# Where the constant rows of attention keys come from, and what stands behind a router on VectorE

## The chip, the core and the metric

One core of a Trainium2 chip runs the whole kernel: TensorE (PE: matmuls, with its weight loads), VectorE (DVE), ScalarE (ACT), GpSimd (POOL), and SyncE (SP), whose queue issues every DMA of this kernel. Inputs lie in DRAM, tiles in SBUF (128 partitions) or in PSUM, where matmuls write. The metric is device time in microseconds (us), the median of several runs; the profile is of one execution.

## The reference: what is computed

Two batches of 256 tokens of width 256 go through four blocks. Each block adds a cross-attention over a context of 4096 tokens, then a self-attention, then a feed-forward part (often experts with a router). The change concerns block 2's end and block 3's cross-attention:

```python
q = split_heads(hidden_states @ q_w.T + q_b)       # 16 heads of 16
k = split_heads(context @ k_w.T + k_b)
v = split_heads(context @ v_w.T + v_b)
scores = einsum('bhqd,bhkd->bhqk', q, k) / sqrt(16)
scores = where(mask, -inf, scores)
ctx = einsum('bhqk,bhkd->bhqd', softmax(scores), v)
```

Block 2's feed-forward part has eight routed experts and two shared ones: the two largest of eight logits per token get softmax gates, the other experts a gate of zero.

## The kernel before

**Two lanes and a planner.** The program is written by two helpers ("lanes"): a on the left of SBUF, x on the right; the trace puts the lane's letter before a tile's name (axn, xk). The order on each engine is not the order of the program: a planner simulates the program on a timeline and puts each instruction where it expects it to be ready; explicit dependencies bind it. `behind` (a method that was there before) adds such a dependency: on the same engine it only orders, across engines it waits. Once planned, each engine runs its queue strictly in order.

**Block 2, batch 1.** `l2_attn` (L1234 its output) stacks keys and queries of heads by small DMAs (L526, the last at 846.74 us), then `l2_ffn` normalizes its output (`layernorm`: statistics L426 and L427, abn_ve L432, a power on GpSimd L417, axn L441), transposes it on TensorE (L449), copies it (axf L468, axnT), multiplies by the router (L1073), and finds the two largest logits and the gates in 19 small VectorE operations (`first_max` L1089 to L1097, up to L1262). `along` turns the gates (L1111) and spreads them over all partitions by way of DRAM (L1115, L1119). Five pairs of experts follow (`glu`: L413, L1028 to L1032, L1132 to L1135), then the output (L1269) and, in `x3_queries`, a second layernorm and the queries of block 3, written to DRAM (q_d).

**Block 3's cross-attention** (`l3_xattn`) works in two passes over the same keys. Keys and values were made earlier and lie in DRAM (kh_d and kl_d, the high and low part of a number in two, and v_d). A group is 4 heads of one batch: 8 groups, each in 4 chunks of 1024 keys, so 32 chunks. A chunk's keys are a tile of 128 partitions by 4 heads by 512: each half of the partitions holds 512 keys of each head, and in each half the 16 dimensions take four rows each: high, high, low, and one more (MASK, row 3 of each four). Of the sixteen rows of this kind in a half, the first (row 3) holds the mask of the keys and the others ones; the query tile has a one against row 3, and, in rows 7 and 11, two parts of minus the row's maximum against ones, so that the matmul itself adds the mask and subtracts the maximum. All other rows of this kind meet a zero in the query tile.

First pass (`max_steps`): per chunk eight times two matmuls into a PSUM tile f of two banks (L1378; two such tiles in turn), and a maximum over each 512 keys on VectorE (L1380, xpm<-xf). After a group's four chunks the maxima are joined (nm), turned and written into the query tile by DMA (`shift_rows`). Second pass (`exponents`): scores again (L1407), exponentials on ScalarE (L1411), times the values (L581). The first pass runs five chunks ahead (`ahead`): 40 maxima stand before the second pass begins, the other 216 are spread over it, eight a chunk. The scores of the second pass use PSUM buffers of the x lane and, in turn, those of lane a, in which block 2's experts and the queries of batch 1 work; the trace's first L1407 comes behind them.

**Tiles.** Seven key tiles (RING) and three query tiles (Q_SETS) are used in turn. `x3_tiles` fills each once: a key tile with ones by a memset on GpSimd (L1300), so that a chunk's loads need to bring only its keys (three loads, L1370) and its mask rows (L1371, row 3 of each half); a query tile with a copy of the column unmask (one in row 3 of each half, else zero) on GpSimd (L1296). Query rows come by six DMAs of 64 KB (L526), three for each half. The first four key tiles and the first query tile lie in a pool on the left (early), where lane a worked on batch 0's experts and queries until then; the others in a pool on the right (late).

`masks` runs in block 1, at about 460 us: it turns the mask into 0 or −1e30 in DRAM (md), spreads it over four heads (mk_d), and writes a small tile of ones to DRAM (fill_d).

Of the kernel before, what the change touches and what calls it, by code (L numbers as in the profile page):

```python
# [28 lines left out]
P = 128  # L29
# [261 lines left out]
class Lane:  # L291
# [231 lines left out]
    def rows_from(self, x, at, n, src, step=1):  # L523

        to = x[at : at + step * (n - 1) + 1 : step].bitcast(F32)
        self.nc.sync.dma_start(to, src.bitcast(F32) if src.dtype == F32R else src)  # L526
# [117 lines left out]
class Perceiver:  # L644
# [528 lines left out]
    def l2_attn(self, k, b, x):  # L1173
# [3 lines left out]
        with k.pool("a2", bufs=1) as ap:  # L1177
# [37 lines left out]
            for g in range(4):  # L1215
# [5 lines left out]
                k.rows_from(k4, k.ADD + 2, 2, sqd[:, g4, :])  # L1221
# [15 lines left out]
    def l2_ffn(self, b, x):  # L1237
# [4 lines left out]
        with k.pool("f2", bufs=2) as fp:  # L1242
# [19 lines left out]
            nc.vector.tensor_add(g8, g8, h2)  # L1262
# [21 lines left out]
    def x3_tiles(self, at):  # L1284


        k, nc = self.x, self.nc
        i, c = divmod(at, self.N_C)

        def tile(tag, n):  # L1290
            return k.t(self.early if at < self.N_C else self.late, [P, GRP, n], tag, F32R, bufs=1)

        if c == 0 and i < self.Q_SETS:

            x = tile(f"q{i}", S)
            nc.gpsimd.tensor_copy(x, self.unmask.unsqueeze(1).to_broadcast([P, GRP, S]))  # L1296
            self.x3_q.append(x)
        if at < self.RING:
            x = tile(f"k{at}", 512)
            nc.gpsimd.memset(x.bitcast(F32), 1.0)  # L1300
            self.x3_k.append(x)
        return self.x3_q[i % self.Q_SETS], self.x3_k[at % self.RING]
# [10 lines left out]
    def masks(self):  # L1313

        k, nc = self.a, self.nc
        with k.pool("mask", bufs=1) as mp:
# [10 lines left out]
            nc.sync.dma_start(self.fill_d, fill)  # L1327

    def x3_queries(self, b, x):
# [3 lines left out]
        with k.pool("x3q", bufs=1) as ap:  # L1333
            xnT = k.transposed(k.layernorm(x, ap), ap, "xnT")
            k.to_dram(k.proj_t_split(wq, xnT, ap, "qT", bias="x3.bq"), self.q_d[b])

    def l3_xattn(self, xs):
# [13 lines left out]

        def max_steps(at):
# [3 lines left out]
            g4 = slice(GRP * g, GRP * g + GRP)  # L1356
            q4, k4 = self.x3_tiles(at)
            if c == 0:
                for h in range(2):
                    at = h * self.HALF  # L1360
                    for r, part in enumerate(k.QUERIES):
                        src = self.q_d[b, part].rearrange("m (h d) n -> d (m h) n", d=HD)
                        k.rows_from(q4, at + r, HD, src[:, g4, :], self.PARTS)
                    if i >= self.Q_SETS:
                        k.rows_from(q4, at + self.SHIFT, 2, self.zeros, self.PARTS)
                state[i] = q4, k.t(self.early, [P, 2, GRP, 2 * n_c], "pm", bufs=2), []
            q4, pm, ks = state[i]
            u2 = slice(2 * c, 2 * c + 2)
            for r, src in ((0, self.kh_d), (1, self.kh_d), (2, self.kl_d)):
                nc.sync.dma_start(k4[r :: self.PARTS].bitcast(F32), src[b, u2, :, g4, :].rearrange("u d j n -> (u d) j n"))  # L1370
            nc.sync.dma_start(k4[self.MASK :: self.HALF].bitcast(F32), self.mk_d[b, u2])  # L1371
            ks.append(k4)
            for j in range(GRP):
                for t in range(2):
# [5 lines left out]
                    nc.vector.tensor_reduce(at, both.rearrange("p (h n) -> p h n", h=2), axis=AX.X, op=ALU.max)  # L1380
# [82 lines left out]
        nc.gpsimd.memset(self.zeros.bitcast(F32), 0.0)  # L1463
        xp = self.late
# [7 lines left out]
        for at in range(ahead):  # L1472
            steps = max_steps(at)
# [6 lines left out]
        for at in range(n):  # L1480
            steps = max_steps(at + ahead) if at + ahead < n else iter(())
# [356 lines left out]
    def run(self):  # L1838
# [15 lines left out]
        self.q_d = a.dram([B, 2, 2, P, S], "q_d")  # L1854
# [6 lines left out]
        self.v_d = a.dram([B, 4, P, L // 512, 4 * GRP * (HD + 1)], "v_d")  # L1861
        self.md = a.dram([B, L], "md")
# [13 lines left out]
        with ExitStack() as wa:  # L1876
            a.wraw = wa.enter_context(a.pool("wraw", bufs=2))
            a.wp = wa.enter_context(a.pool("w", bufs=4))
            with ExitStack() as early:
# [3 lines left out]
                with self.psum(x, mm=2, s=2, pr=1), self.psum(a, mm=3), x.pool("wraw", bufs=1) as x.wraw, x.pool("w", bufs=2) as wp, x.pool("xq", bufs=1) as self.xq:  # L1883
# [37 lines left out]
                    xb[1] = self.l2_attn(x, 1, xb[1])  # L1921
                x.p_bufs = 3
# [51 lines left out]
```

## Time and profile before

| what | us |
|---|---|
| median of 3 runs (lowest, highest) | 1518.61 (1515.18, 1522.23) |
| the profiled execution's own time | 1513.83 |
| its span, first to last instruction | 1512.1 |
| busy in the span: PE, DVE, ACT, POOL | 1353.1, 1108.8, 891.4, 521.0 |
| L1380, 256 maxima: busy, mean of one | 310.2, 1.234 |
| output of block 2's attention, batch 1 (L1234 begins) | 863.10 |
| first and last L1380 begin | 870.4, 1230.2 |
| first L1407 begins | 951.7 |

The page gives, of one execution, each engine's busy time; then the chain of waits, followed back from the last instruction, whose shares say what the end hung on. The timeline lists instructions of an engine in order of time: start, duration (of several merged ones, their whole stretch), engine, line, operation, output and input, and in brackets how long the engine sat idle before and for whom. A table by stretches gives, for each, its length and each engine's busy time (PE, PEld, DVE, ACT, POOL) with the number of instructions, the granted TensorE clock (1.00 is full speed), the share of time in which the 16 DMA engines were busy, and GB/s. An instruction that straddles two stretches counts in both numbers, its time only where it falls.

### The profile page before, as it was taken

How to read it: one execution, taken by the hardware profiler on the slowest of the kernel's cores; microseconds unless marked ns; L12 is line 12 of the kernel's file. 1: busy time of each engine (PE TensorE's matmuls, PEld its weight loads, DVE VectorE, ACT ScalarE, POOL GpSimd, SP SyncE). 2: the span in 40 equal slices, each digit the busy share in tenths (PEclk: the TensorE clock that was granted, in tenths of full speed). 3: DMA queues.
4: the chain of work that ended last, by engine and by line, in shares of the span. 5: the costliest groups of instructions: out<-in, count | busy, mean ns of one | idle time of the engine just before them, and what ended most of it. 6: DMA issues, size and time to landing. Idle time of an engine off the chain costs nothing.

```text
span 1512.1 us, 29306 instructions
## 1 busy us (share of the span) xinstructions
PE 1353.1 (89%) x11278; PEld 1108.8 (73%) x11278; DVE 1108.8 (73%) x1863; ACT 891.4 (59%) x1644; POOL 521.0 (34%) x397
## 2 busy tenths in 40 slices
PE   7898788979998999998998767899999998987698
PEld 6898778969998998998898436455555544774588
DVE  6999855446467878885588599799999961566675
ACT  6676555637775655764664303688888897233243
POOL 6755344335445544664335413000000001531130
PEclk9999999979999999999999959899999999986799
DMA  8754164556455556445642542333333312300262
GB/s 288 250 152 131 33 190 161 184 172 217 149 177 169 176 177 214 146 155 179 164 128 89 172 165 95 121 119 109 126 122 107 113 53 61 136 1 30 84 218 75
DMA packets 125143, 212.00 MB, mean 140 GB/s; under 512 B 12840, under 2 KB 89240, under 8 KB 121480
## 3 DMA queue, kind: packets, MB, share of 16 engines
q1 hardware_dynamic: 125004, 210.13, 44.1%
q8 instruction: 89, 1.46, 0.4%
q14 instruction: 50, 0.41, 0.1%
HBM read 181.32 MB, written 28.61 MB: 139 GB/s over the span
## 4 chain that ended last, share of the span: by engine, by line
PE 48%; DVE 14%; ACT 5%; DMA 4%; POOL 4%; issue 3%; SPq 1%; POOLq 0%; DVEq 0%; ACTq 0%
PE amm L413 9%; PE xacc L581 7%; PE xmm L413 6%; PE xf L1378 5%; DVE xpm L1380 4%; PE xs L413 4%; PE xpr L413 4%; DMA awr<-in_w 2%; PE amm L1407 2%; POOL aw L406 2%; ACT xp L1409 1%; PE xmm L788 1%; PE amm L1796 1%; PE xs L1407 1%; PE amm L581 1%
## 5 line engine op out<-in xcount | busy, mean ns | idle before, releaser
L1380 DVE TENSOR_REDUCE xpm<-xf 128x2 f32<-128x1024 f32 x256 | 310.2, 1234 | 7.5 <-PE xf L1378 5.9
L1411 ACT ACTIVATE xp<-amm 128x512 f32<-128x512 f32 x284 | 162.0, 595 | 29.6 <-PE amm L1407 17.6
L406 POOL TENSOR_TENSOR aw<-awr,aw 128x1024 fp32r<-128x1024 f32 (+1 forms) x53 | 126.5, 2389 | 148.2 <-ACT aw L404 114.8
L404 ACT CAST aw<-awr 128x1024 fp32r<-128x1024 f32 (+1 forms) x112 | 114.0, 1021 | 99.8 <-DMA awr<-in_w 60.3
L413 PE MATMUL xmm<-xvx,xpT 128*128 128x256 f32 x1152 | 167.2, 291 | 2.8 <-DVE xo L801 1.3
L581 PE MATMUL xacc<-xp,xv 128*17 128x256 f32 x2048 | 161.0, 387 | 4.1 <-DVE xot L1430 1.1
L413 PE MATMUL xs<-xkx,xqkT 128*128 128x256 f32 x1152 | 162.1, 285 | 2.7 <-POOL xkx L738 1.9
L738 POOL TENSOR_TENSOR xvx<-xraw,xvx 128x512 fp32r<-128x512 f32 x96 | 131.9, 1389 | 89.6 <-ACT xvx L736 89.1
L1378 PE MATMUL xf<-xk,xq 64*128 64x512 f32 x512 | 135.8, 527 | 22.2 <-DVE xpm L1380 13.6
L413 PEld LDWEIGHTS xmm<-xvx,xpT 128*128 128x128 f32 x1152 | 147.9, 193 | 6.0 <-DVE xo L804 2.0
L413 PEld LDWEIGHTS xs<-xkx,xqkT 128*128 128x128 f32 x1152 | 147.6, 191 | 4.6 <-POOL xkx L738 2.1
L1378 PEld LDWEIGHTS xf<-xk,xq 64*128 64x128 f32 x512 | 51.1, 196 | 124.1 <-issue 83.2
L407 DVE TENSOR_TENSOR aw<-awr,aw 128x1024 fp32r<-128x1024 f32 (+1 forms) x59 | 86.6, 1473 | 60.9 <-ACT aw L404 60.8
L1445 POOL TENSOR_TENSOR ax<-xou,xmh_ri 128x128 f32<-128x128 f32 x8 | 3.2, 402 | 315.9 <-DVE xmh_ri L1441 315.9
L413 PE MATMUL amm<-axnT,aw 128*128 128x256 f32 x636 | 98.9, 313 | 10.2 <-ACT axnT L404 5.5
L413 PE MATMUL amm<-ah,aw 128*128 128x256 f32 x768 | 99.6, 286 | 6.0 <-ACT au L1013 2.9
L413 PEld LDWEIGHTS amm<-axnT,aw 128*128 128x128 f32 x636 | 91.3, 217 | 17.8 <-ACT axnT L404 7.2
L413 PEld LDWEIGHTS amm<-ah,aw 128*128 128x128 f32 x768 | 94.7, 191 | 8.7 <-POOL aw L406 3.7
L738 POOL TENSOR_TENSOR xkx<-xraw,xkx 128x512 fp32r<-128x512 f32 x48 | 72.1, 1503 | 82.9 <-ACT xkx L736 82.3
L1411 ACT ACTIVATE xp<-xs 128x512 f32<-128x512 f32 x148 | 88.0, 595 | 11.3 <-PE amm L1407 7.8
L1407 PE MATMUL amm<-xq,xk 64*128 64x256 f32 x568 | 89.3, 283 | 3.0 <-DVE aqT L402 2.7
L777 ACT ACTIVATE xp<-xs,xnm 128x512 f32<-128x512 f32 x96 | 66.2, 690 | 34.8 <-DVE xnm L771 32.6
(603 smaller groups left out, 2920.6 us busy)
## 6 DMA issues: line engine op xcount, KB each, us to landing
awr<-in_w SPq DMA_DIRECT2D x105, 512.0 KB
xraw<-in_ctxT SPq DMA_DIRECT2D x108, 256.0 KB
xraw<-in_ctx SPq DMA_DIRECT2D x96, 256.0 KB
xk<-akh_d SPq DMA_DIRECT2D x64, 256.0 KB
av_d<-xkvv SPq DMA_DIRECT2D x16, 544.0 KB
xv<-av_d SPq DMA_DIRECT2D x32, 272.0 KB
akh_d<-xkvk SPq DMA_DIRECT2D x32, 256.0 KB
akl_d<-xkvk SPq DMA_DIRECT2D x32, 256.0 KB
```

Source lines behind the costliest of these rows:

```text
L404: nc.scalar.copy(dst.h, src)
L406: return lo.tensor_tensor(dst.l, src, dst.h.bitcast(F32), ALU.subtract)
L407: return nc.vector.tensor_sub(dst.l, src, dst.h)
L413: tie(self.nc.tensor.matmul(out, lhsT=x, rhs=y, start=start and i == 0, stop=stop and i == 2))
L581: inst = self.nc.tensor.matmul(acc[STRIP * j : STRIP * j + v(j).shape[1], :S], lhsT=v(j), rhs=p[:, j, :], start=start, stop=stop)
L738: nc.gpsimd.tensor_tensor(x.l, r, x.h.bitcast(F32), ALU.subtract)
L777: tie(nc.scalar.activation(p, score.pop(i), AF.Exp, bias=least[q], accum_out=su))
L788: tie(nc.tensor.transpose(pst[:, t * P : (t + 1) * P], p[:, t * P : (t + 1) * P], self.eye))
L1378: tie(nc.tensor.matmul(both[:, h * 512 : (h + 1) * 512], lhsT=q4[rows, j, t * P : (t + 1) * P], rhs=k4[rows, j, :], start=True, stop=True))
L1380: nc.vector.tensor_reduce(at, both.rearrange("p (h n) -> p h n", h=2), axis=AX.X, op=ALU.max)
L1407: tie(nc.tensor.matmul(ps[h][:, j, :], lhsT=ks[c][rows, a + j, s * P : (s + 1) * P], rhs=q4[rows, a + j, :], start=True, stop=True))
L1411: exps = [nc.scalar.activation(p[:, h, a : a + 2, :], ps[h], AF.Exp, scale=0.25) for h in range(2)]
```

## The change

Key tiles are no longer filled on GpSimd. A DRAM array mo_d holds, for the 4 chunks of batch 0, all 16 rows of the fourth kind: mask in the first, ones in the other 15; `masks` writes it by two more DMAs. Chunks that use a key tile for the first time (the first seven) load these 32 rows of 8 KB instead of the two mask rows. The copy into the query tiles goes from GpSimd to ScalarE.

The loads of keys get a function of their own, `load_keys`; for the first four chunks it is called before the first pass is set up (a first `yield None`, which `run` takes with `next(l3)` right after batch 1's attention of block 2), with an order: behind the last stacking DMA of that attention (`self.stacked`). The maxima of chunk 0 get an order behind the last addition of the gates (`self.gated`, of the latest `l2_ffn`, batch 1's), on the same engine.

The queries' array in DRAM is laid out by dimension, head and token, so that `x3_queries` writes it by four DMAs instead of one, and each part of a query tile is read by one DMA for both halves (three instead of six).

```diff
 l2_attn:
-                k.rows_from(k4, k.ADD + 2, 2, sqd[:, g4, :])
+                self.stacked = k.rows_from(k4, k.ADD + 2, 2, sqd[:, g4, :])
 l2_ffn:
-            nc.vector.tensor_add(g8, g8, h2)
+            self.gated = nc.vector.tensor_add(g8, g8, h2)
 x3_tiles:
-            nc.gpsimd.tensor_copy(x, self.unmask.unsqueeze(1).to_broadcast([P, GRP, S]))
+            nc.scalar.copy(x, self.unmask.unsqueeze(1).to_broadcast([P, GRP, S]))
...
-            x = tile(f"k{at}", 512)
-            nc.gpsimd.memset(x.bitcast(F32), 1.0)
-            self.x3_k.append(x)
+            self.x3_k.append(tile(f"k{at}", 512))
 masks:
+            n_u = 2 * self.N_C
+            nc.sync.dma_start(self.mo_d[:, 0], self.md[:1, : n_u * 512].rearrange("a (u n) -> (a u) n", n=512).unsqueeze(1).to_broadcast([n_u, GRP, 512]))
+            ones = self.fill_d[:1, :].unsqueeze(1).to_broadcast([n_u, HD - 1, GRP * 512])
+            nc.sync.dma_start(self.mo_d[:, 1:].rearrange("u d j n -> u d (j n)"), ones)
 x3_queries:
-            k.to_dram(k.proj_t_split(wq, xnT, ap, "qT", bias="x3.bq"), self.q_d[b])
+            qT = k.proj_t_split(wq, xnT, ap, "qT", bias="x3.bq")
+            for m in range(2):
+                for r in range(2):
+                    dst = self.q_d[b, r, :, HEADS // 2 * m : HEADS // 2 * (m + 1), :].rearrange("d h n -> h d n")
+                    self.nc.sync.dma_start(dst, qT.both[:, r, m, :].bitcast(F32))
 l3_xattn:
-        def max_steps(at):
+        def load_keys(at):
             b, g, c, i = place(at)
             q4, k4 = self.x3_tiles(at)
             if c == 0:
                 state[i] = q4, k.t(self.early, [P, 2, GRP, 2 * n_c], "pm", bufs=2), []
+            g4, u2 = slice(GRP * g, GRP * g + GRP), slice(2 * c, 2 * c + 2)
+            loads = []
+            for r, src in ((0, self.kh_d), (1, self.kh_d), (2, self.kl_d)):
+                loads.append(nc.sync.dma_start(k4[r :: self.PARTS].bitcast(F32), src[b, u2, :, g4, :].rearrange("u d j n -> (u d) j n")))
+            if at < self.RING:
+                loads.append(nc.sync.dma_start(k4[self.MASK :: self.PARTS].bitcast(F32), self.mo_d[u2].rearrange("u d j n -> (u d) (j n)")))
+            else:
+                nc.sync.dma_start(k4[self.MASK :: self.HALF].bitcast(F32), self.mk_d[b, u2])
+            if at < n_c:
+                for x in loads:
+                    k.behind(x, self.stacked)
+            state[i][2].append(k4)
+        def max_steps(at):
...
+                for r, part in enumerate(k.QUERIES):
+                    src = self.q_d[b, part, :, g4, :].unsqueeze(0).to_broadcast([2, HD, GRP, S])
+                    nc.sync.dma_start(q4[r :: self.PARTS].bitcast(F32), src)
...
-                    nc.vector.tensor_reduce(at, both.rearrange("p (h n) -> p h n", h=2), axis=AX.X, op=ALU.max)
+                    found = nc.vector.tensor_reduce(at, both.rearrange("p (h n) -> p h n", h=2), axis=AX.X, op=ALU.max)
+                    if b == g == c == 0:
+                        k.behind(found, self.gated)
...
+        for at in range(n_c):
+            load_keys(at)
+        yield None
```

## The prediction

> **What bounds the kernel now.** I read the page first (busy shares, chain), then the chain in order of time, then the stretch between block 2's attention on batch 1 and the steady loop of block 3, engine by engine.
>
> ```profile
> PE 1353.1 (89%) x11278; PEld 1108.8 (73%) x11278; DVE 1108.8 (73%) x1863; ACT 891.4 (59%) x1644; POOL 521.0 (34%) x397
> ...
> PE 48%; DVE 14%; ACT 5%; DMA 4%; POOL 4%; issue 3%; SPq 1%; POOLq 0%; DVEq 0%; ACTq 0%
> ```
>
> TensorE carries the chain over the whole, but POOL holds 4% of it. In order of time, its POOL pieces between 845 and 882 us are L1300 and L1296, from 859.0 to 873.7, but for 0.5 us: the fillings that the change removes. The same stretches by engine (busy us and instructions, then granted clock, DMA share, GB/s):
>
> ```profile
> 863.80:873.80 10.00, 1.32 (x4) 0.63 (x4) 9.88 (x7) 0.00 (x0) 9.91 (x9) 0.64 0.85 281
> 873.80:884.40 10.60, 7.33 (x20) 2.83 (x20) 9.75 (x11) 0.00 (x0) 0.70 (x1) 0.50 0.75 250
> 884.40:902.00 17.60, 12.39 (x40) 6.14 (x38) 17.37 (x35) 1.28 (x3) 0.00 (x0) 0.50 0.31 109
> 902.00:920.00 18.00, 16.35 (x96) 12.57 (x96) 16.02 (x18) 5.48 (x8) 3.68 (x2) 0.84 0.27 89
> 920.00:938.80 18.80, 16.68 (x109) 13.78 (x110) 18.03 (x23) 5.14 (x9) 6.59 (x4) 0.91 0.24 74
> 938.80:955.80 17.00, 7.75 (x40) 5.89 (x39) 7.49 (x14) 5.96 (x8) 5.40 (x3) 0.79 0.41 125
> ```
>
> The third busy column is VectorE. It is full from 863.8 to 938.8 us, but its first 10 us do nearly nothing (7 instructions), and from 938.8 to 955.8 every engine is below half. Its lines:
>
> ```profile
> 864.83 8.91 DVE L432 TENSOR_SCALAR abn_ve<-abn_mv 128x2 f32<-128x2 f32 x1
> 870.44 3.31 DVE L1380 TENSOR_REDUCE xpm<-xf 128x2 f32<-128x1024 f32 x2
> ...
> 883.71 0.73 DVE L441 TENSOR_SCALAR axn<-ax,abn_mv,abn_rs 128x256 f32<-128x256 f32 x2
> ...
> 901.68 0.17 DVE L1262 TENSOR_TENSOR ag<-ag,agh 128x16 f32<-128x16 f32 x1
> ```
>
> And GpSimd's:
>
> ```profile
> 858.98 7.03 POOL L1300 MEMSET xk<- 128x2048 f32 x4
> 865.96 0.56 POOL L627 MEMSET xot<- 128x256 f32 x2
> 866.47 1.03 POOL L1296 CAST xq<-ac_unmask 128x1024 fp32r<-128x1024 f32 x1
> 867.45 5.28 POOL L1300 MEMSET xk<- 128x2048 f32 x3
> 872.69 1.03 POOL L1296 CAST xq<-ac_unmask 128x1024 fp32r<-128x1024 f32 x1
> 873.82 0.70 POOL L417 TENSOR_TENSOR abn_rs<-abn_ve,amhalf 128x2 f32<-128x2 f32 x1
> ```
>
> Batch 1's layernorm for block 2's experts needs abn_ve (VectorE, two numbers a row), then a power on GpSimd (L417), then axn. abn_ve takes 8.91 us; the same instruction took 0.17 at 944.98. It ends with GpSimd's last filling (873.7). The power stands behind the fillings in GpSimd's queue anyway. By 873.8 the plan of the program has ten first maxima (L1380) ahead of axn, so axn is done at 884.4 instead of about 866.6; then each of the routing's small operations alternates with a maximum of 1.2 us, and the gates (L1262) are ready at 901.85. The experts follow (output at 940.84), then batch 1's queries, and the steady loop:
>
> ```profile
> 946.48 1.18 PE L449 MATMUL amm<-ac_eye,axn 128*128 128x128 f32 x4 [5.67 <-issue]
> 948.33 3.44 PE L413 MATMUL amm<-axnT,aw 128*128 128x256 f32 x12 [0.67 <-ACT axnT L404]
> 951.70 0.51 PE L1407 MATMUL amm<-xq,xk 64*128 64x256 f32 x1
> 954.92 0.50 PE L1407 MATMUL amm<-xq,xk 64*128 64x256 f32 x3 [2.71 <-DVE aqT L402]
> ```
>
> So two things must be finished before the loop can run (exponents, L1407): batch 1's experts and queries (whose PSUM buffers the scores reuse), and 32 of the 40 first maxima with their row shift. The maxima were finished by 938.8 and the experts were late: that is what the change can win, VectorE's idle time from 938.8 to 955.8.
>
> **Part by part.**
>
> *Fillings gone from GpSimd.* 7 memsets of 1.794 and 3 copies of 1.026: 15.6 us of GpSimd, and with them the wait of abn_ve and of the power. The Trainium skill, "SBUF — State Buffer", section "Who interferes with whom", names the cause: a tensor_scalar can take both ports, which GpSimd shares, and the second to come blocks for one whole instruction of the other. Here it blocked through the rest of one GpSimd instruction and seven more, 8.91 us, where by that rule it would be at most one, 1.79, and abn_ve alone would lose 7 us less. The sum needs no rule for it: the power's place in GpSimd's queue alone sets 873.8.
>
> *Routing runs alone.* By rows of this stretch: output of the attention 863.8; statistics to 864.8; abn_ve 0.17; power 0.70; axn 0.73, so 866.6; four transposes 1.1; copy on ACT 0.58; logits 1.88 (L1073); sum of these with gaps 870.2. Then 19 small VectorE operations that follow each other at 0.20 us (888.57 to 889.2), 3.8, and one exponential on ACT (0.20) with two handovers, about 0.7; with the gaps, gates at **874.9** instead of 901.85.
>
> *Maxima behind the gates.* The wait is on the eight maxima of chunk 0, but all others use the same two PSUM buffers (f), so all 40 stand behind 874.9. Behind the waiting maximum on VectorE stand the later maxima; on TensorE the third pair of their matmuls. Nothing else that could run is lost if the planned order puts the routing in front, which the dependency enforces on VectorE. What is lost are the 23 maxima that before ran up to 901.8. Their price: eight in a row take 9.14 us (874.65 to 883.79), 1.14 each; beside others 1.22. I take 1.18: 27.1 us.
>
> *The sum.* After the gates, VectorE before had 16.02 + 18.03 + 7.49 = 41.5 us of work up to the loop. After the change: 41.5 + 27.1 = 68.6 from 874.9, so 943.5 with no idle time. From 902 to 938.8 it idled 36.8 − 34.05 = 2.8; with as much, 946.3. I round to **946** for the state that before was reached at 955.8: 10 us won. Check on the other need: gates to output took 39.0 before, output to last query 14.1; from 874.9 that is 928. The 32nd maximum comes eight (9.1 us) before the end, 937; its shift (nm, split, transposes, ACT copy, DMA: 0.22 + 0.5 + 0.4 + 0.4 + two issues of 0.65 and about 2 to land) gives 942, so exponents begin while the last four maxima run. VectorE sets the end, not the chain.
>
> *Rows of ones by DMA.* A chunk's keys are three loads of 256 KB and 16 KB of mask (L1371); now the fourth load is 32 rows of 8 KB, 256 KB: 1.68 MB more for seven chunks, at the 322 to 341 GB/s of 865.9 to 873.8 some 5 us of a queue that is already 0.95 busy there. But keys no longer wait for fillings: the tiles' space comes free when batch 0's queries are in DRAM (855.4, where GpSimd's zeros waited for that write), against first loads at 864.0 before. Four chunks, 4.2 MB, take 12.6 us at 332 GB/s: 868 to 870. Maxima need them from 874.9: nothing, as long as TensorE's queue does not hold the routing behind them (first rival).
>
> *Moves with one answer, nothing:* q fillings on ACT (three of about 1.03, as L404's 128x1024 copies; ACT idles from 860 to 885.7); q_d written by four DMAs instead of one (three more issues of 0.38 on SP, which idles from 849.8 to 854.4); queries read by three DMAs instead of six (SP saves about 1.8 us a group; no wait for SP stands in the loop's chain).
>
> *mo_d is written at about 467 us*: two issues (0.70 each, as mk_d's) and 1 MB, between 0 (TensorE 9.45 of 10 busy, loads ahead) and 4.5 us (1.4 of issue and 3.1 of DMA, since one raw load was waited for 5.3 us there). I take **1**.
>
> *Clock.* TensorE idles from 863.1 to 869.5 before and was granted 0.61, then 0.50 up to 902; after, it again has little to do up to 874.9, then the experts' dense matmuls sooner. A pair of maxima's matmuls took 0.80 at 0.50, less than a maximum. Nothing. The Trainium skill, "TensorE: Matmul & The Clock Gate", section "What's actually happening", says a few us of idleness halve the clock and as much sustained work restores it; by it the expert matmuls of the first 3.4 us would take double, an estimate of 1.7 us against the change.
>
> Net 9: 1513.83 − 9 = 1504.8 on the profiled execution's scale (span 1512.1 and 1.7 around it). That execution lies 4.8 below the median 1518.61; I predict on the median's scale: **1509.6**.
>
> **Rivals.**
>
> *Late queries.* If q's loads are issued behind the four chunks' keys, they land at about 870.5 (868.0, 1.2 for 0.39 MB, and the landing); if TensorE's planned order has the first two pairs of maxima's matmuls (1.3) ahead of the routing's transposes, these start at 871.8 instead of 866.5 and the gates come at 880: 5 of the 9 lost, 1515. For it: the 25.9 us that axf's wait is put down to xk's load show that the routing stood behind the maxima before. Against: the planner now knows that they wait.
>
> *Given back.* VectorE's idle time only moves, or the loop waits for chunks 5 and 6, whose keys are 30% larger, or mo_d costs its 4.5: 1518. Against: seven chunks were in by 890 before; loop loads come a chunk ahead.
>
> *Slower: experts without maxima between.* Expert and query work comes first in the program, and if the plan lets it run alone, 40 maxima start late. Batch 0's experts and queries took 47 us from gates (802.4) to the write at 849.4: from 874.9 that is 922, then 32 maxima at 1.14 and 5 of shift: 963.5 against 954.9, with mo_d's 1: 9.6 slower, 1528. It decides when VectorE idles over 12.4 us (943.5 to 955.8) between the gates and the loop. Against: before, maxima alternate with every expert operation.
>
> **Numbers.** Forecast 0.58, late queries 0.18, given back 0.10, slower 0.14. Half a per cent (7.6 us) is about what a measurement of this kernel can tell from no change. Of the forecast 0.46 lies beyond it and 0.12 within; late queries and given back lie within; of the slower 0.12 beyond. Faster 0.46, same 0.42, slower 0.12. The range runs from all idle time used and none lost, 1513.8 − 12.4 = 1501, to 1521, which takes in "given back" and leaves out most of the slower case.
>
> **What would show it.** abn_ve at 0.2 us; no POOL work from 857 to 865 but a weight split; gates near 875 with no L1380 before them; L1380 without gaps from there; L1407 begins near 942; the last L1380 9 to 10 us earlier than 1231.4. Wrong if gates come after 885, if VectorE shows idle gaps over 12 us before the loop, or if the loop's maxima take longer each than now (275.2 us for 216).

## The result, and the profile after

The changed kernel is slower. Its median is 1542.07 us (1539.89 to 1545.36, four runs) against 1520.42 for the kernel before on the same chip: a ratio of **1.015**, 95% interval 1.0114 to 1.0185. A second measurement (e16) gave 1.0155, 1.0132 to 1.0178. The forecast was 1509.6 with a range up to 1521.

The profiled execution took 1543.79 us (span 1542.0). First the page after, its busy times and its chain:

```profile
PE 1364.2 (88%) x11278; PEld 1114.7 (72%) x11278; DVE 1103.6 (72%) x1863; ACT 896.0 (58%) x1647; POOL 506.6 (33%) x387
...
PE 43%; DVE 16%; DMA 9%; ACT 5%; issue 3%; POOL 3%; SPq 1%; POOLq 0%; DVEq 0%; ACTq 0%
```

GpSimd has 14.4 us less to do and VectorE 5.2 less, as the fillings' removal should give; TensorE has 11 more for the same 11278 matmuls (its granted clock is 0.93 over the whole, before 0.94). DMA has gone from 4% of the chain (6% in a second profile of before, e15) to 9% (9% in e16 too): more of the end hangs on transfers. The other shares say little, since two profiles of one kernel differ as much (PE 48% and 60% in the two of before).

The stretches that answer to those shown of before, in the same columns (the attention's tail in two rows, the routing, the experts' start, a hole, the experts, and the last of the forty first maxima):

```profile
846.00:864.00 18.00, 15.73 (x111) 9.15 (x110) 8.46 (x22) 9.30 (x17) 2.02 (x2) 1.00 0.49 138
864.00:878.50 14.50, 10.65 (x46) 6.46 (x46) 3.53 (x6) 5.33 (x8) 0.30 (x1) 0.69 0.93 334
878.50:895.20 16.70, 4.39 (x17) 2.99 (x16) 8.12 (x29) 4.21 (x6) 3.61 (x4) 0.50 0.68 225
895.20:908.50 13.30, 12.43 (x74) 10.11 (x74) 12.00 (x13) 3.88 (x6) 0.00 (x0) 0.81 0.59 192
908.50:922.20 13.70, 0.50 (x2) 0.19 (x2) 0.00 (x0) 0.41 (x1) 1.28 (x2) 0.57 0.39 136
922.20:953.20 31.00, 26.75 (x148) 21.49 (x148) 26.72 (x28) 8.37 (x11) 10.90 (x6) 0.80 0.24 65
953.20:980.60 27.40, 16.91 (x56) 8.32 (x56) 26.06 (x35) 3.78 (x6) 3.04 (x2) 0.66 0.31 95
```

The fifth row is the new thing: for 13.7 us hardly any engine computes (GpSimd 1.28 us, at the end), and DMA is busy only 0.39 of the time. VectorE's rows in the timeline say what stands around it:

```profile
880.29 0.17 DVE L432 TENSOR_SCALAR abn_ve<-abn_mv 128x2 f32<-128x2 f32 x1
881.27 2.78 DVE L441 TENSOR_SCALAR axn<-ax,abn_mv,abn_rs 128x256 f32<-128x256 f32 x2 [0.82 <-DMA arow_f2.br<-in_rows]
...
894.98 0.17 DVE L1262 TENSOR_TENSOR ag<-ag,agh 128x16 f32<-128x16 f32 x1
895.15 2.36 DVE L1399 TENSOR_REDUCE xpm<-xf 128x2 f32<-128x1024 f32 x2
...
907.26 1.21 DVE L1399 TENSOR_REDUCE xpm<-xf 128x2 f32<-128x1024 f32 x1
922.22 0.69 DVE L1135 TENSOR_TENSOR au<-amm,ag 128x512 f32<-128x512 f32 x1 [13.74 <-POOL ag L1134]
```

The routing did what was forecast: abn_ve takes 0.17 instead of 8.91, the gates (L1262) come 15.9 us after the attention's output (879.2) instead of 38.1, with no maximum (L1399 now) ahead of them. Then VectorE waits 13.74 us for GpSimd's L1134, the multiplication of an expert's output by its gates. The gates go to all partitions by way of DRAM: SP's write L1115 and, once it has landed, its reads L1119. Of the kernel before, and then of the kernel after with the GpSimd and TensorE instructions that wait (two timelines):

```profile
904.46 0.30 SPq L1115 DMA_DIRECT2D agates<-agrow  x1
905.78 0.81 SPq L1119 DMA_DIRECT2D agates<-agates  x2
```

```profile
906.51 0.39 SPq L1115 DMA_DIRECT2D agates<-agrow  x1
916.46 0.81 SPq L1119 DMA_DIRECT2D agates<-agates  x2
920.92 1.26 POOL L1134 TENSOR_TENSOR ag<-ag,agates 128x512 f32<-128x512 f32 x1 [37.01 <-DMA agates<-agates]
922.96 2.29 PE L413 MATMUL amm<-axnT,aw 128*128 128x256 f32 x9 [13.92 <-DVE au L1135]
```

Before, 1.3 us lie between issuing the 8 KB write and issuing the reads that need it; after, 10.0. The write is also issued 11.4 us after L1262 (before 2.6): SP's queue still had loads of keys, values and queries ahead of it.

**Where the time went.** Both kernels were profiled twice (e15 and e16 are unchanged copies). Means of two profiles, us, by the same landmarks:

| stretch | before | after | difference |
|---|---|---|---|
| start to masks (L1324, L1322) | 468.8 | 473.1 | +4.3, the same work in both |
| masks to the end of block 2's attention on batch 0 (L1234) | 318.6 | 323.3 | +4.7 |
| to the end of the same on batch 1 | 77.8 | 83.0 | +5.2 |
| to the steady loop of block 3 (first L1407, now L1429, that writes lane x's score buffers, xs) | 91.7 | 102.4 | +10.7 |
| to the last maximum | 275.7 | 275.3 | −0.4 |
| to the end | 279.4 | 281.4 | +2.0 |

The first row is not put down to the change: up to there every engine runs the same instructions in the same order in both kernels, and over all eighteen profiles this point lies anywhere from 465.7 to 475.1, with no clear relation to the edits. The three rows in the middle are the question. (The very first L1407 writes a buffer of lane a, a little earlier; the table of before gives that one, 951.7. Counted to it, the way from the attention takes 87.9 before and 101.3 after.)

### The profile page after: what moved, and what is told of

Same layout as the page of the kernel before. It is cut to its first block, busy times and chain, and to the rows that moved or that the text cites. A ratio compares the mean times of both kernels' runs of the same rounds, so it can differ in the third digit from the quotient of the medians.

```text
span 1542.0 us, 29272 instructions
## 1 busy us (share of the span) xinstructions
PE 1364.2 (88%) x11278; PEld 1114.7 (72%) x11278; DVE 1103.6 (72%) x1863; ACT 896.0 (58%) x1647; POOL 506.6 (33%) x387
## 4 chain that ended last, share of the span: by engine, by line
PE 43%; DVE 16%; DMA 9%; ACT 5%; issue 3%; POOL 3%; SPq 1%; POOLq 0%; DVEq 0%; ACTq 0%
PE xacc L581 7%; PE amm L413 7%; PE xf L1397 5%; PE xmm L413 5%; DVE xpm L1399 5%; PE xs L413 3%; PE xpr L413 3%; DMA awr<-in_w 3%; PE amm L1429 2%; POOL aw L406 1%; ACT xp L1431 1%; PE xmm L788 1%; PE xs L1429 1%; DVE aw L407 1%; ACT aw L404 1%
## 5 line engine op out<-in xcount | busy, mean ns | idle before, releaser
L1399 DVE TENSOR_REDUCE xpm<-xf 128x2 f32<-128x1024 f32 x256 | 309.1, 1220 | 5.7 <-PE xf L1397 3.9
L1433 ACT ACTIVATE xp<-xs 128x512 f32<-128x512 f32 x148 | 88.0, 595 | 11.4 <-PE amm L1429 8.3
L1429 PE MATMUL amm<-xq,xk 64*128 64x256 f32 x568 | 88.8, 284 | 0.0
```

The costliest lines, as they stand in the source:

```text
L1399: found = nc.vector.tensor_reduce(at, both.rearrange("p (h n) -> p h n", h=2), axis=AX.X, op=ALU.max)
L1429: tie(nc.tensor.matmul(ps[h][:, j, :], lhsT=ks[c][rows, a + j, s * P : (s + 1) * P], rhs=q4[rows, a + j, :], start=True, stop=True))
L1433: exps = [nc.scalar.activation(p[:, h, a : a + 2, :], ps[h], AF.Exp, scale=0.25) for h in range(2)]
```

## The experiments

Ratios are against the kernel before on the same chip, with 95% intervals. The table holds stretches of each profile in us: A from masks to attention 0's end, B from there to attention 1's end, then abn_ve, the gates after attention 1's end with the maxima ahead of them, the write-to-read time of the gates (L1115 to L1119), and the loop after attention 1's end. A maximum counts as ahead when it begins before the record of the gates' last addition ends; the single one of e3, e8 and e11, where the order holds, begins within that record's last 0.1 us. Each profile is of one execution, which can lie several us off its run's median (e5's 7.3 and e7's 9.9 under it).

| run | ratio | A | B | abn_ve | gates (maxima ahead) | L1115 to L1119 | loop |
|---|---|---|---|---|---|---|---|
| before | 1 | 319.0 | 78.2 | 8.91 | 38.1 (24) | 1.3 | 91.6 |
| e15 before, again | 0.9993 [0.9978, 1.0009] | 318.2 | 77.4 | 8.83 | 38.0 (24) | 1.3 | 91.8 |
| after | 1.015 [1.0114, 1.0185] | 323.2 | 83.5 | 0.17 | 15.9 (0) | 10.0 | 102.5 |
| e16 after, again | 1.0155 [1.0132, 1.0178] | 323.4 | 82.5 | 0.17 | 16.2 (0) | 10.3 | 102.3 |
| e1 before, mo_d written | 1.0033 [1.0016, 1.005] | 322.1 | 79.2 | 8.22 | 37.4 (24) | 1.3 | 91.3 |
| e2 after, chunks 4 to 6 later | 1.0093 [1.0063, 1.0123] | 324.2 | 80.9 | 0.17 | 16.2 (0) | 10.1 | 94.7 |
| e3 before, order | 1.0039 [1.0021, 1.0058] | 321.0 | 77.3 | 7.89 | 17.2 (1) | 1.7 | 92.6 |
| e4 after, no order | 1.0062 [1.0038, 1.0086] | 323.3 | 81.8 | 0.17 | 28.6 (14) | 7.0 | 89.4 |
| e5 before, fillings behind gates | 1.0027 [1.0004, 1.0051] | 317.6 | 78.9 | 0.17 | 18.4 (8) | 1.3 | 88.5 |
| e6 before, fillings behind axn | **0.9962** [0.9941, 0.9983] | 317.3 | 77.3 | 0.17 | 22.7 (13) | 1.6 | 83.9 |
| e7 after, no order, no mo_d, old query path | 1.0013 [0.9988, 1.0039] | 318.1 | 78.1 | 0.85 | 23.4 (7) | 2.6 | 89.5 |
| e8 after, old query path | 1.0051 [1.0032, 1.007] | 323.7 | 77.3 | 0.85 | 17.7 (1) | 5.1 | 88.8 |
| e9 after, query reads by halves | 1.0035 [1.0018, 1.0052] | 321.9 | 83.3 | 0.17 | 11.9 (0) | 4.0 | 84.9 |
| e10 before, new query path | 1.0033 [1.0018, 1.0049] | 320.3 | 81.0 | 3.35 | 32.3 (24) | 1.3 | 86.9 |
| e11 = e6 and the order | 1.002 [1.0003, 1.0038] | 319.9 | 77.2 | 0.17 | 13.4 (1) | 1.6 | 86.4 |
| e12 before, ScalarE fills | 1.0037 [1.0016, 1.0059] | 315.6 | 85.7 | 0.17 | 23.0 (17) | 1.3 | 83.3 |
| e13 = e9 without mo_d | 1.0022 [1.0004, 1.0039] | 319.6 | 82.4 | 0.17 | 15.8 (0) | 1.6 | 88.1 |
| e14 = e9 without the order | 1.0 [0.9983, 1.0018] | 321.1 | 83.7 | 0.17 | 24.1 (14) | 1.3 | 83.5 |

**e1_written: mo_d's price.** Before, and `masks` also writes mo_d, which nobody reads.

```diff
 masks:
+            nc.sync.dma_start(self.mo_d[:, 0], self.md[:1, : n_u * 512].rearrange("a (u n) -> (a u) n", n=512).unsqueeze(1).to_broadcast([n_u, GRP, 512]))
+            ones = self.fill_d[:1, :].unsqueeze(1).to_broadcast([n_u, HD - 1, GRP * 512])
+            nc.sync.dma_start(self.mo_d[:, 1:].rearrange("u d j n -> u d (j n)"), ones)
```

> The kernel before, with the array mo_d allocated and written in block 1 as in the change, and read by nobody. Four-places theory (the change loses some 10 us by 490 us, 5 us at the end of block 2's attention and 19 us at the gates' spreading, and wins 22 at the routing): writing mo_d costs 3 to 4 us at about 480 us, and if the array's place in DRAM is what slows the weight loads from 250 us on, 7 more: 1520.4 + 3 to 10, so 1523 to 1531. Order theory (the loss is VectorE held idle, since first maxima may not run ahead of the gates): nothing here, 1520.

It cost 0.33%, 5.0 us (2.4 to 7.6). Most of it can be seen at one place. ScalarE and TensorE of before, and then of e1:

```profile
480.81 0.62 ACT L736 CAST xkx<-xraw 128x512 fp32r<-128x512 f32 x1 [5.25 <-DMA xraw<-in_ctxT]
482.27 1.69 PE L413 MATMUL xpr<-xw,xkx 128*128 128x256 f32 x12 [2.67 <-ACT xkvv L386]
```

```profile
485.94 0.62 ACT L736 CAST xkx<-xraw 128x512 fp32r<-128x512 f32 x1 [8.42 <-DMA xraw<-in_ctxT]
487.41 2.93 PE L413 MATMUL xpr<-xw,xkx 128*128 128x256 f32 x12 [5.84 <-ACT xkvv L386]
```

The load of context that before came 5.25 us late comes 8.42 late; TensorE idles 3.2 longer, and its next twelve matmuls take 1.2 longer (granted clock 0.65 from 484 to 490 us, before 1.00 there and from 479 to 485). Stretch A averages 322.9 in the eight profiles with mo_d (321.1 to 324.2) and 318.7 in the ten without (315.6 to 321.0): 4.2 us.

**e2_gates_first: are the later key loads in the gates' way?** After, and the key loads of chunks 4 to 6 stand behind the gates' reads.

```diff
+            elif at < self.RING:
+                for x in loads:
+                    k.behind(x, self.spread)
```

> The changed kernel, with the loads of chunks 4, 5 and 6 ordered on SP behind the DMA that spreads batch 1's gates. Four-places theory: the gates' way through DRAM falls from 23 us (897.8 to 920.9) to about 8, TensorE's gap of 13.9 us at 909 goes, 14 us won: 1528. Order theory: VectorE is as idle before the gates as in the change, and the maxima are as late: 1540 to 1542.

The write is issued sooner (2.7 us after the gates instead of 11.4), and 0.57% comes back. But its readers still follow 10.1 us later, with no key load around it: the packets in flight in that time are the queries', two at a time (e9 shows how to tell them). So the key loads explain when the write is issued, not how long it takes.

**e3_order_only and e4_no_order: the order.** Before with the order of the first maxima added, and after with it taken out.

```diff
-            nc.vector.tensor_add(g8, g8, h2)
+            self.gated = nc.vector.tensor_add(g8, g8, h2)
...
-                    nc.vector.tensor_reduce(at, ...)
+                    found = nc.vector.tensor_reduce(at, ...)
+                    if b == g == c == 0:
+                        k.behind(found, self.gated)
```

> The kernel before, with only the order of chunk 0's maxima behind the gates; GpSimd's fillings stay, keys and queries come as before. Four-places theory: abn_ve still ends with the fillings (873.7), then the routing runs alone, gates at about 884 instead of 901.9; 68.6 us of VectorE's work and 3 idle end at 955, where the loop began before: 1517 to 1523. Order theory: VectorE loses some 10 us before the gates and gives them to nobody: 1530 or more.

> The changed kernel without the order of the maxima behind the gates. Four-places theory: maxima may run between the routing's operations again, but keys and queries are still loaded ahead of the gates' spreading, so the 10, 5 and 19 us stay: 1536 to 1546. Order theory: the loss goes, 1520 to 1525.

By itself the order brings the gates 21 us forward (17.2 us after the attention instead of 38.1, though abn_ve still takes 7.89), and all of it is given back: the loop comes 92.6 us after the attention, before 91.7; the time is 0.39% longer. Without it, the changed kernel wins 0.9%. So neither of the two theories stated with e1 holds alone: the order has a price, and with it gone 0.62% of loss is left.

**e5_fill_later and e6_fill_behind_axn: keep the fillings, but out of the way.** Before, and GpSimd's fillings of all tiles but the first of each kind stand behind the gates (e5), or behind axn (e6, whose diff for the keys is shown; e5 has self.gated for self.normed, and the copies into the query tiles are treated alike); nothing else of the change.

```diff
-            nc.gpsimd.memset(x.bitcast(F32), 1.0)
+            fill = nc.gpsimd.memset(x.bitcast(F32), 1.0)
+            if at:
+                k.behind(fill, self.normed)
```

> The kernel before; GpSimd's fillings of key tiles 1 to 6 and query tiles 1 and 2 stand behind batch 1's gates (a wait across engines), the maxima have no order. If the fillings' hold on abn_ve and on the power is what delays the routing: abn_ve 0.2 us, chunk 0's eight maxima run in the routing's gaps, gates near 879 instead of 901.9, and 59 us of VectorE's work with 6 idle end near 945 instead of 955.8: about 10 us under before, ratio 0.993. Rival (chunk 1's tile is filled too late and VectorE waits for it as long as it wins): ratio 1.00.

> As e5_fill_later, but the fillings stand behind axn, the last step of the layernorm, not behind the gates: chunk 1's tile is filled some 12 us earlier, and the maxima go on between the routing's operations, as before. Fillings theory: abn_ve 0.2 us, gates near 882, 8 to 10 us under before, ratio 0.994. Rival (maxima between the routing's operations delay the gates to nearly 900 whatever comes first): ratio 0.998 to 1.00.

e6 beats both kernels: 0.9962, 5.8 us (2.6 to 8.9). That is the part of the forecast that holds. abn_ve takes 0.17, and the fillings run while VectorE does something else. Its routing is not alone (13 maxima run between), yet the loop comes 7.8 us sooner than before. e5, with 8 maxima in the routing, has its loop 3.2 sooner; its time, 0.27% over before, shows nothing of it, and why is not known.

**e7_no_mo_q_back and e8_q_back: the query path.** e8 is after with the old layout of q_d, its one write, the six reads of a group and GpSimd's copy into the query tile. e7 does without the order and mo_d as well (ones come straight from the small tile of ones).

```diff
-                    src = self.q_d[b, part, :, g4, :].unsqueeze(0).to_broadcast([2, HD, GRP, S])
-                    nc.sync.dma_start(q4[r :: self.PARTS].bitcast(F32), src)
+                for h in range(2):
+                    row = h * self.HALF
+                    for r, part in enumerate(k.QUERIES):
+                        src = self.q_d[b, part].rearrange("m (h d) n -> d (m h) n", d=HD)
+                        k.rows_from(q4, row + r, HD, src[:, g4, :], self.PARTS)
```

> The changed kernel without the order of the maxima, without mo_d (the rows of ones come straight from fill_d, two more DMAs a chunk, and the mask rows as before), and with queries written, filled and read as before. Four-places theory: without the 5 us of mo_d and the 3 to 5 at the end of block 2's attention what e4_no_order won from the attention's output on remains: 3 us under before, ratio 0.998. Order theory: the same as e4_no_order, 1.006.

> The changed kernel, with only the query path as before: q_d written by one DMA, read by six, query tiles filled on GpSimd. Four-places theory: the attention's last group no longer waits behind four writes on SP and a filling on ACT, 3 to 5 us less than the changed kernel, ratio 1.012. Order theory: no difference, 1.015.

e8 takes the loss from 1.5% to 0.51%, more than either theory expected: the query path, which the forecast cost at nothing, makes two thirds of it. e7 is level with before.

**e9_q_halves: only the reads.** After, and each part of the queries is read by two DMAs, one for a half, with the 16 dimensions outermost.

```diff
-                    src = self.q_d[b, part, :, g4, :].unsqueeze(0).to_broadcast([2, HD, GRP, S])
-                    nc.sync.dma_start(q4[r :: self.PARTS].bitcast(F32), src)
+                    for h in range(2):
+                        k.rows_from(q4, h * self.HALF + r, HD, self.q_d[b, part, :, g4, :], self.PARTS)
```

> The changed kernel with one thing put back: each part of a query tile is read by two DMAs, one for each half, with the 16 dimensions outermost, instead of one DMA whose outermost dimension is a broadcast of two. The layout of q_d, its four writes, ScalarE's fillings, mo_d and both orders stay. Theory (the broadcast of two confines a read to two DMA engines, and the gates wait behind them): the gates' way through DRAM takes under 6 us instead of 9.9, the idle 13.7 us of PE and DVE before the first gate multiplication shrink by at least 5, and the kernel is some 10 us under the changed one: 1.004 to 1.009. Rival (the layout, the four writes and ScalarE's filling make the 15 us that the query path cost): 1.012 to 1.018, as the change itself.

1.0035 instead of 1.015: the form of these reads alone costs 1.15%, some 17 us. The trace's records of packets show how. DMA packets in flight at one moment, with their size in bytes:

```
us       after                      us       e9
908.0    8 of 2176                  898.0    13 of 4096, 1 of 16384
910.0    2 of 4096                  900.0    16 of 4096
912.0    2 of 4096                  901.0    13 of 4096
914.0    2 of 4096                  902.0    16 of 4096, 1 of 4
```

The queries' packets are 4096 bytes (those of 2176 belong to the values). After, two are in flight at nearly every moment from 909 until 916, with nothing else moving; e16 repeats it. In e9's column the weights and the gates' own spreading, packets of 4096 bytes too, are mixed in. Later, in the loop, the 96 packets of a group's queries are the only ones of that size: the changed kernel has two of them in flight, for moments three, through 7.6 us (1027.97 to 1035.61), and e9 up to fifteen. The read's outermost dimension is the broadcast of two halves, and **only two of the sixteen DMA engines work on it**. The Trainium skill, "DMA: Bandwidth & Descriptors", section "Rules for kernel authors", says just this: the number of engines comes from the slowest dimension that is not one, so an outermost broadcast of c copies keeps a DMA on at most c engines. The trace agrees, with its two, and it shows the other half of the damage: what is issued later waits behind. Three such reads of a group are issued three times between 875 and 906; the gates' 8 KB write has its readers only 10 us after its issue. Its eight packets, of 1024 bytes, show that it is these two engines that hold it up: before, all eight are done between 905.27 and 905.41; after, six by 908.35 and the last two at 915.61 and 915.86, when the last query packet ends (915.82). In e16, e2 and e4 two of the eight come late in the same way. In e9, SP and GpSimd:

```profile
891.70 0.43 SPq L1115 DMA_DIRECT2D agates<-agrow  x1
895.71 0.80 SPq L1119 DMA_DIRECT2D agates<-agates  x2
901.56 1.27 POOL L1134 TENSOR_TENSOR ag<-ag,agates 128x512 f32<-128x512 f32 x1 [20.08 <-DMA xq<-aq_d]
```

4.0 us instead of 10.0, and VectorE waits 0.89 us for the first L1134 instead of 13.74. And with that, the gates come 11.9 us after the attention (forecast: 11.1) and the loop 84.9 (forecast: 82.2). The time is no longer than e8's (1.0051), though e9 keeps the four writes and ScalarE's fillings and its stretch B is 6.0 us longer: the loop comes 3.9 us sooner after the attention.

**e10_q_path: the same path in the kernel before.** Before with the new layout, the four writes and the three broadcast reads; fillings as before.

```diff
-        self.q_d = a.dram([B, 2, 2, P, S], "q_d")
+        self.q_d = a.dram([B, 2, HD, HEADS, S], "q_d")
```

> Before with only the change's query path: q_d by dimension and head, four writes, three broadcast reads for a group (the filling stays on GpSimd, and no order, no mo_d). Theory: the reads run on two DMA engines here too; three groups are read while the routing runs, so the gates' way through DRAM takes 6 us or more instead of 1.3: 8 to 15 us, 1.005 to 1.010. Rival (the reads hurt only where the order holds the maxima back and lets all loads come in one burst): 0.999 to 1.003.

1.0033: less than I expected, and at the upper end of the rival. Here the reads are issued while the maxima run, the last at 898.5, and the gates' write at 911.1: the last of their packets is done by 910 (1.3 us from write to read). So the reads do harm when the gates' write meets them in flight. The order makes this worse, but it is not needed: e4 and e14 differ only in the form of these reads, both without the order, and e4 takes 0.62% longer (1.0062 against 1.0000; 7.0 us from write to read against 1.3, the loop 5.9 us later). With the order the same difference is 1.15% (after against e9).

**e11_axn_and_order: the forecast's sum in a clean setting.** e6 with the order, by the same three lines as in e3.

> Before, with the later fillings of GpSimd put behind axn of block 2's layernorm (the version that ran at 0.996) and, on top, the change's order of the first maxima behind batch 1's gates. It is the forecast's sum without mo_d and without the new query path. The forecast's sum: gates 11 to 16 us after the attention's output, 68.6 us of VectorE work and 3 idle behind them, loop about 10 us sooner than before: 0.992 to 0.995, and the last maximum 9 to 10 us earlier relative to the attention's output. Rival (what the routing wins, the maxima that no longer run between its operations give back): as the version without the order, or up to 5 us over it: 0.996 to 1.001.

The first half of the sum holds: gates 13.4 us after the attention. The second does not: the loop comes 86.4 us after it, against 83.9 without the order, and the time is 1.002 against 0.9962. By stretches (attention to gates, to the experts' output, to the loop), of e6 and of e11:

```profile
860.50:883.20 22.70, 12.57 (x40) 6.29 (x40) 18.00 (x40) 1.28 (x3) 13.20 (x9) 0.50 0.80 275
883.20:927.40 44.20, 37.26 (x228) 28.86 (x228) 39.89 (x47) 12.92 (x18) 12.67 (x7) 0.93 0.35 107
927.40:944.30 16.90, 9.72 (x34) 5.94 (x35) 13.44 (x20) 3.56 (x6) 3.04 (x2) 0.60 0.27 90
```

```profile
864.80:878.20 13.40, 4.25 (x16) 3.09 (x16) 6.19 (x28) 1.28 (x3) 11.30 (x8) 0.50 0.87 304
878.20:923.10 44.90, 38.50 (x224) 30.34 (x224) 39.92 (x43) 12.50 (x17) 15.00 (x9) 0.86 0.46 153
923.10:951.20 28.10, 19.17 (x61) 9.63 (x61) 26.76 (x35) 4.27 (x8) 3.04 (x2) 0.53 0.27 91
```

The third busy column is VectorE. With the order it does 6.19 us of work in the routing's 13.4, without it 18.0 in 22.7: the 9.3 us won in the first stretch are lost again, 11.2 in the last, where VectorE (26.76 of 28.1 busy) still works off maxima.

**e12_fill_act: fillings on ScalarE.** Before, and all fillings go to ScalarE.

```diff
-            nc.gpsimd.memset(x.bitcast(F32), 1.0)
+            for j in range(0, GRP, 2):
+                nc.scalar.activation(x[:, j : j + 2, :], self.unmask.rearrange("p (a n) -> p a n", a=1)[:, :, :1].to_broadcast([P, 2, 512]), AF.Copy, scale=0.0, bias=1.0)
```

> Before with the key and query tiles filled by ScalarE instead of GpSimd, nothing else. If GpSimd's fillings cost what the profile of before shows (abn_ve 8.9 us, the power behind them), and ScalarE has room between 860 and 885 us: abn_ve 0.2 us, 0.994 to 0.998. Rival (ScalarE's fillings, 14 of about 1 us and three more, now stand in the way of the attention's last exponentials and of the routing's copies): 0.998 to 1.003.

Slower, 1.0037. The routing gains as in e6 (loop at 83.3), but stretch B grows by 8. ScalarE's timeline shows the fillings in front of the attention's own copies:

```profile
857.22 1.04 ACT L1296 CAST xq<-ac_unmask 128x1024 fp32r<-128x1024 f32 x1 [0.23 <-DMA aq_d<-aqT]
858.16 7.67 ACT L1301 ACTIVATE xk<-ac_unmask 128x1024 fp32r<-128x1024 f32 x8
865.74 0.56 ACT L404 CAST xxnT<-xpr 128x512 fp32r<-128x512 f32 x1
```

**e13_halves_no_mo and e14_halves_no_order: what is left of e9's 5 us.** e9 without mo_d (ones straight from the small tile, mask from mk_d), and e9 without the order.

> The changed kernel with query reads by halves (the version that ran at 1.0035) and, on top, without mo_d: the rows of ones come straight from the small tile of ones in DRAM by two more loads a chunk, the mask from mk_d as before. The order behind the gates stays. If mo_d's writing makes what is left of the loss: 0.998 to 1.001, and the stretch up to 490 us loses the 5 us. If the order makes it: 1.003 to 1.005.

> The changed kernel with query reads by halves and without the order of the first maxima behind the gates; mo_d stays. If the order makes what is left of the loss: 0.998 to 1.001. If mo_d's writing makes it: 1.003 to 1.005, with maxima between the routing's operations again and the loop no later.

Without mo_d stretch A falls by 2.3 us and the time to 1.0022, an interval that overlaps e9's; but chunks then need two more loads each, and the gates come 4 us later. Without the order the time is that of before, 1.0000, as expected if the order makes what is left: it costs 0.35% here too, and the loop is 1.4 us sooner without it. That does not make mo_d free: e14 still pays for it, and by e1 (5.0) and e6 (5.8) that is about what it wins by having no fillings in the way; this sum is argued, no run shows it.

**e15_before_again and e16_after_again: controls.** Unchanged copies.

> The kernel before, unchanged, as one more kernel: 0.999 to 1.001. Its second profile shows how far the same instructions drift from one execution to another. If block 2's attention on batch 1 ends within 3 us of 863.8 again, the 13 us by which the versions without an early cause are late there come from the changes; if it ends anywhere up to 875, they are run-to-run.

> The changed kernel, unchanged, once more and against the same runs of before as the others: 1.012 to 1.018. Its second profile must show the gates' way through DRAM at 8 us or more and some 13 us of idle TensorE and VectorE before the first gate multiplication, if these come from the queries' reads and not from one execution's accident; if they come from an accident, it shows them below 4 us.

Attention 1 ends at 866.6 in e15 (863.8 in the first profile) and at 879.6 in e16 (879.2): the changed kernel is late there again, by 13.0 us (15.4 in the first pair), of which on average 4.3 lie ahead of the masks and are not put down to the change. So does the wait for the gates, e16:

```profile
906.87 0.31 SPq L1115 DMA_DIRECT2D agates<-agrow  x1
917.17 0.81 SPq L1119 DMA_DIRECT2D agates<-agates  x2
921.52 1.26 POOL L1134 TENSOR_TENSOR ag<-ag,agates 128x512 f32<-128x512 f32 x1 [36.93 <-DMA agates<-agates]
```

## Why the prediction was wrong, step by step

**Fillings gone from GpSimd: right.** abn_ve 0.17, the power not queued. e6 shows what it is worth to have the fillings out of the way: 7.8 us up to the loop, 5.8 in time. abn_ve's long stay came again in the second profile of before (8.83), where the rule of the Trainium skill, "SBUF — State Buffer", section "Who interferes with whom", as the prediction gave it, would have it wait for one instruction of GpSimd.

**Routing runs alone: nearly right.** Gates 11.1 us after the attention were forecast; 15.9 were measured. 3.9 of the difference is the mechanism of the rival "late queries": TensorE's queue held the first maxima's matmuls ahead of the logits, and these waited for the queries.

```profile
888.94 1.22 PE L1397 MATMUL xf<-xk,xq 64*128 64x512 f32 x4 [3.93 <-DMA xq<-aq_d]
890.09 1.88 PE L1073 MATMUL amm<-acols,axf 128*128 128x8 f32 x8
```

With reads that use all engines (e9) the gates came after 11.9. That the keys would be there in time was right: in the changed kernel, from 879 to the loop, no maximum's matmul waits for a load of keys, and only the one shown for queries. The granted clock was 0.50 in the routing and in the 3.4 us behind the gates (895.2 to 898.6), and 0.81 over the experts' start; what that costs, no run isolates.

**Maxima behind the gates: the equation was right, the gain was not the order's.** From the gates to the loop the sum gave 68.6 us of VectorE work and 2.8 idle. e9 has 73.1 us there, 66.3 of them busy; the loop comes 6.8 us sooner than before relative to the attention, of 10 forecast (4.1 by the very first L1407). But e14, without the order, comes 8.2 sooner. Four pairs (e3 and before, e4 and after, e11 and e6, e14 and e9) agree in sign: the order costs 0.35 to 0.9% of the time. VectorE is the engine that limits this stretch, so running the routing alone leaves it idle (7 of 13.4 us in e11), and the experts that start sooner find it full of maxima later. What VectorE gains is that abn_ve no longer blocks it, and that needs no order. The price in time of the order, 5 to 9 us in e9 and e11, is larger than the 1.4 to 2.5 us that its profiles show up to the loop; where the rest lies stays open.

**"Moves with one answer, nothing": the step that failed.** *Queries read by three DMAs instead of six* counted issues on SP, and not how many engines each one uses: it costs 1.15% (after against e9), seen in the trace as the 13.7 us hole and the routing's 3.9. *q_d written by four DMAs, fillings on ScalarE*: I counted SP idle from 849.8 to 854.4, behind q_d's one write, and 0.38 us for each further one; but the planner put the four writes, 3.55 us, ahead of the attention's last two stacking loads, which before stood ahead of the write. SP of the kernel before, and then SP, TensorE and ScalarE of the kernel after:

```profile
846.74 0.25 SPq L526 DMA_DIRECT2D xk<-xa2s  x1
...
849.38 0.38 SPq L521 DMA_DIRECT2D aq_d<-aqT  x1
```

```profile
857.89 3.55 SPq L1341 DMA_DIRECT2D aq_d<-aqT  x4
861.49 0.44 SPq L526 DMA_DIRECT2D xq<-xa2s  x1
861.98 0.25 SPq L526 DMA_DIRECT2D xk<-xa2s  x1
...
864.46 0.71 PE L574 MATMUL xs<-xq,xk 128*128 128x256 f32 x4 [0.71 <-DMA xk<-xa2s]
...
864.12 1.04 ACT L1296 CAST xq<-ac_unmask 128x1024 fp32r<-128x1024 f32 x1 [3.14 <-DMA aq_d<-aqT]
865.07 1.78 ACT L575 ACTIVATE xp<-xs 128x512 f32<-128x512 f32 x3
```

From the end of batch 0's attention, the last of these loads goes out 61.2 us later before and 66.2 after: 5.1 us, about what stretch B grew by. ScalarE, too, waits 3.14 us for q_d's writes before its filling, with the attention's exponentials (L575) behind; but their scores are not made before 864.46, so this filling holds them by some tenths of a us. Stretch B averages 82.6 in the seven profiles with both edits and 77.9 in the nine with neither: 4.7 us. In e10, with the four writes but GpSimd's fillings, the writes (3.04) stand ahead of the loads too, and B is 81.0.

**mo_d: mis-sized.** Between 0 and 4.5 were given, 1 was taken; 5.0 (2.4 to 7.6) was measured, 4.2 by stretch A. The upper bound was the better figure. It was made of the load that was already waited for there, and that is where the time went (8.42 for 5.25); that TensorE was busy, my ground for the lower end, did not protect it.

**The sum.** mo_d 4.7, the attention's tail 5.2, attention to loop 10.7 (the blocked time won, and more than that lost by the hole): 20.6, beside the measured 23.5 (20.0 to 27.0). Of the rivals, "experts without maxima between" had the right sign but less than half the size (9.6 us slower, 1528), and its mark (VectorE idle over 12.4 us between gates and loop) came true by another cause: the experts waited for their gates, and not for their own chain. For e9 the same rows give 3.3 + 5.5 − 6.8 = 2.0, where 5.3 (2.7 to 7.9) was measured: about 3 us there stay open.

## What to carry to other kernels

Count the DMA engines that a transfer's outermost dimension can use, as well as its issues: a broadcast put outermost turns fewer DMAs into a slow one, and small transfers that others wait for then stand behind it. Before giving one chain the right of way on an engine, ask whether that engine limits the stretch: if it does, an order only moves its idle time. If a filling is in the way, first try to run it a few us later (e6); here, moving it to another engine (e12) or to DMA (mo_d) brought a bill there.

## What was not expected of the hardware

- A read of 128 KB with a broadcast of two outermost kept two packets of 4096 bytes in flight; an 8 KB write issued behind such reads had its readers about 10 us later instead of 1.3.
- A megabyte written from DRAM to DRAM in block 1 cost 5.0 us of the whole, though nothing waited for it (e1).
- VectorE's axn (two TENSOR_SCALAR) took 2.78 us after and 0.73 before; its second half began 0.04 us after GpSimd's weight split (881.57 to 883.91) and ended 0.15 behind it, and the same 2.45 us stand in e2, e9 and e14. So the removal of fillings did not end such blocking, and here it lasted for one GpSimd instruction.
